# Layer 1 of a two-layer graph network: head 0's product of tile 29 through logs on ScalarE and GpSimd

## The chip, the cores and the metric

The kernel runs on one core of a Trainium2 chip. The metric is the device time of one launch in microseconds; lower is better. The engines are named as in the profile: PE (TensorE, with PEld for its weight loads), DVE (VectorE), ACT (ScalarE), POOL (GpSimd) and SP (SyncE, which here only issues transfers).

## The reference

There are 4096 nodes with 512 features, and an adjacency matrix `adj` of zeros and ones, 4096 x 4096, all in fp32. Layer 0 is a graph attention whose scores come from `h @ h.T`. Layer 1, which the change touches, has 8 heads of 64 features:

```
h = relu(layernorm(x))
data1 = (h @ W.T + b).reshape(N, 8, 64)
src = sum over d of data1 * src_proj          # one number per node and head
trg = sum over d of data1 * trg_proj
e = src[n] + trg[m]                           # per head
e = where(e >= 0, e, 0.01 * e)
e = e + adj[n, m]
scores = softmax over m of e
out[n] = sum over m of scores[n, m] * data1[m]
x = x + out
```

So a term of the softmax, before it is divided by its sum, is `exp(adj) * exp(leaky(src + trg))`.

## The kernel before

Layer 0 takes roughly the first 1.6 ms, and layer 1 the rest. In layer 1 the scores are kept transposed: neighbours `m` on the 128 partitions, nodes `n` along the free dimension, 1024 at a time (`WL`). A *group* is 1024 nodes and four of the eight heads (`HG`), so there are eight groups, 0 to 7. Inside a group the loop runs over 32 *tiles* of 128 neighbours. The order of all work is written out by hand: step `s` of the loop at the end of the kernel calls the functions in `stages`, each for a tile some steps ahead, and every engine does its instructions in the order in which they are issued.

For each tile:

- `load` (SP) fetches the 128 x 1024 block of `adj.T` into one of four buffers `e`, four steps ahead.
- `exps` (ACT, L1316) writes `exp(adj)` into `ex`, a single buffer in PSUM. It can start only when the last product of the tile before has read it.
- `last_exps` (ACT, L1326) writes `e3`, the same exponential with head 3's factor of the neighbour as bias, into SBUF.
- `weigh` (DVE) makes the products, one per head, in the order 3, 0, 1, 2 (`ORDER`). Heads 1, 2 and 3 are `max(z, g) * ex` (L1379; head 3 with `e3` in place of `ex`). Head 0 is `(rl - ngd) * ex` (L1376), where `rl` is a Relu by ACT (`relus`, L1352). Each product goes into one of two buffers of its head; head 0 has three.
- In the tiles of `BY_LOG` head 0 has no product on DVE. ACT writes the logarithm of the row factor, a Relu, into a single row buffer `lg` (`logs`, L1332); POOL adds `adj` to it in two halves of 512 columns (`add_logs`, L1341); ACT takes the Exp of that with the neighbour's factor as bias, which is head 0's product (`relus`, L1349). The first half is issued on POOL after head 3's sum two tiles earlier; the second half is issued one tile earlier and waits for head 3's product of that tile.
- The softmax's denominators: POOL adds head 3's products into `acc` (L1390). Head 0's products are added into two sums by DMAs that POOL issues (`sums`, L1360 and L1362), except in the tiles of `BY_HALF`, where POOL adds one half itself (L1396) and PE the other. Heads 1 and 2 go to PE.
- `gather` (PE) multiplies the products with the values (`pv`, L1413; first heads 3 and 0, then heads 1 and 2) and adds denominators (`dn`, L1418). At the last tile of a group it also reads the finished sums.

In groups 0 and 1 ACT also scales the values (`scale`, L1312), for the first three tiles POOL does so (L1310). In the first two thirds of a group the results of the group before are turned by PE (`pt`, L1477 and L1496), scaled by ACT and sent out.

Within a step of the loop POOL gets its work from `weigh` in this order: the DMA for the sum of the tile before, the second half of the next tile's logs, head 3's sum, the first half of the logs two tiles ahead, and the half sum of a `BY_HALF` tile. ACT gets `ex`, `e3`, then the Relu or the Exp, then the logs four tiles ahead, then the scaling.

Of the kernel before, what the change touches and what calls it, by code (L numbers as in the profile page):

```python
# [28 lines left out]
def kernel(  # L29
# [657 lines left out]
    def slot(name):  # L687
        n = taken.get(name, 0)
        taken[name] = n + 1
        return slots[name][n % len(slots[name])]  # L690
# [541 lines left out]


    PARTS = (0, 1, 2, 4, 5, 6, 8, 9, 10, 12, 13, 14, 16, 17, 18, 22)
    BY_LOG = (3, 7, 11, 15, 19, 23, 27, 31)
    BY_HALF = (4, 8, 12, 16, 20, 24, 28)
    BY_DMA = [m for m in range(NT - 1) if m not in BY_HALF]
    after = mybir.DependencyInfo(mybir.DependencyClass.Sync, mybir.DependencyReason.DATA)
# [4 lines left out]
    with tile_pool("rl") as rlp, tile_pool("zb") as zp1, tile_pool("ac") as acp, tile_pool("s1") as sp, tile_pool(  # L1243
# [85 lines left out]
        def logs(i, m, early=False):  # L1329
            if m in BY_LOG and early == (m == BY_LOG[0]):  # L1330
                r = lg_row
                nc.scalar.activation(r, us[i], AF.Relu, bias=nlg_m[:, groups[i][1], m:m + 1], scale=-(1.0 - SLOPE))  # L1332
                rl[i, m] = r

        def early_logs(i, m):
            logs(i, m, True)

        def add_logs(i, m, half, behind=None):
            if m in BY_LOG:
                cs = slice(half * BL, (half + 1) * BL)  # L1340
                add = nc.gpsimd.tensor_tensor(rl[i, m][:, cs], rl[i, m][:, cs], ra[i, m][:, cs], ALU.add)  # L1341
                if behind is not None:
                    tc.add_manual_dep(add.ins, behind.ins.name, after, reason="behind head 3's product")

        def relus(i, m):
            h = groups[i][1] * HG
            if m in BY_LOG:
                pr[i, m, 0] = slot("pr0")
# [245 lines left out]
        for s in range(len(steps)):  # L1594
            for f, ahead in stages:
                if s + ahead < len(steps):
                    f(*steps[s + ahead])
                if s == 0 and f is exps:
                    early_logs(0, BY_LOG[0])
            if s == 0:  # L1600
# [45 lines left out]
```

## Time and profile before

| | |
|---|---|
| median of 3 runs | 2763.91 us (2760.75 to 2765.06) |
| profiled execution | 2766.16 us |
| its span, first to last instruction | 2764.3 us |
| granted TensorE clock | 0.999 |
| PE busy | 2743.6 us (99%) |
| DVE busy | 2469.7 us (89%) |
| ACT busy | 1543.1 us (56%) |
| POOL busy | 1441.4 us (52%) |
| from 2025.9 to 2172.4 us (one group's length): DVE, ACT, POOL busy | 145.87, 120.74, 125.63 of 146.5 us |

Times in the profile are microseconds from the span's start. A row of the timeline gives the start, the duration, the engine, the line of the kernel, the operation, and output and inputs by the tile names in memory; several rows that follow one another are merged and counted (x2). A bracket at the end tells how long the engine was idle before it and what ended that. Many buffers of layer 1 reuse memory of layer 0, so their rows carry old names: `he_t`, `at`, `pr` and `ux` are products, Relus and adjacency blocks, `racc` the row of `src`, `rm`, `mb` and `acc_z` columns of factors. Matmuls overlap, so PE's busy time says little; the distance between their starts says more.

In the chain of waits, shares are those of the chain that ended last; "issue" is time in which an engine waited for nothing that the profile shows.

### The profile page before, as it was taken

The numbers are of one execution on the slowest core, as the hardware profiler recorded it, in microseconds if no ns is written. First come the engines' busy times: TensorE is split into PE (matmuls) and PEld (weight loads), VectorE is DVE, ScalarE is ACT, GpSimd is POOL, SyncE is SP. The second block draws the span as 40 slices with busy tenths as digits, with TensorE's granted clock in tenths as the row PEclk, the third lists the DMA queues.
The fourth block names the chain that finished last, engine by engine and source line by source line (L and its number), as shares of the span: only waits on it lengthen the run. The fifth ranks groups of instructions, "written<-read, shape, count | busy, mean of one in ns | idle before, by whom it ended". The sixth has DMA issues, their size and how long they took to land.

```text
span 2764.3 us, 49117 instructions
## 1 busy us (share of the span) xinstructions
PE 2743.6 (99%) x17903; PEld 1777.5 (64%) x17903; DVE 2469.7 (89%) x3362; ACT 1543.1 (56%) x2498; POOL 1441.4 (52%) x1236
## 2 busy tenths in 40 slices
PE   8999999999999999999999999999999999999999
PEld 5885444445888888888885433565656565655555
DVE  5767789899988888888886799999999999999998
ACT  5522233333233333433433588988888888888886
POOL 5313434444010010111108588888889897979797
PEclk9999999999999999999999999999999999999999
DMA  6627898988999999999967489999999998989897
GB/s 197 190 75 289 283 325 300 311 297 264 214 208 197 198 263 193 229 256 211 231 190 190 164 202 244 235 224 247 225 243 225 243 234 238 229 239 231 215 222 173
DMA packets 537122, 632.10 MB, mean 229 GB/s; under 512 B 292184, under 2 KB 346488, under 8 KB 536880
## 3 DMA queue, kind: packets, MB, share of 16 engines
q1 hardware_dynamic: 463600, 419.28, 50.5%
q0 software_dynamic: 71776, 206.81, 34.7%
q8 instruction: 140, 2.29, 0.3%
q10 hardware_dynamic: 1504, 2.88, 0.3%
q14 instruction: 102, 0.84, 0.1%
HBM read 406.33 MB, written 107.15 MB: 186 GB/s over the span
## 4 chain that ended last, share of the span: by engine, by line
PE 82%; DVE 7%; issue 3%; DMA 2%; POOL 2%; SPq 2%; ACT 1%; DVEq 0%; POOLq 0%; ACTq 0%
PE pv L1413 28%; PE po L841 23%; PE pe L585 12%; PE dn L1418 8%; PE bank L297 6%; DVE he_t L1379 2%; PE po L977 2%; SPq L768 2%; PE pt L1496 1%; DMA et<-er_d 1%; POOL a L989 1%; DMA a<-in_adj_t_dram 1%; PE bank L230 1%; DVE at L812 1%; PE bank L237 0%
## 5 line engine op out<-in xcount | busy, mean ns | idle before, releaser
L1413 PE MATMUL pv<-he_t,sup 128*32 128x512 f32 x6488 | 988.5, 592 | 0.9 <-DVE he_t L1379 0.9
L1413 PEld LDWEIGHTS pv<-he_t,sup 128*32 128x32 f32 x6488 | 431.8, 110 | 313.9 <-issue 111.8
L1418 PE MATMUL dn<-he_t,acc_z 128*2 128x512 f32 x1984 | 412.7, 592 | 0.0
L585 PE MATMUL pe<-he_t,he_t 128*128 128x512 f32 x896 | 386.2, 592 | 0.0
L802 ACT ACTIVATE d<-d 128x1024 f32<-128x1024 f32 x126 | 133.1, 1057 | 427.2 <-DVE d L794 226.4
L1316 ACT ACTIVATE ex<-he_t 128x1024 f32<-128x1024 f32 x255 | 262.0, 1027 | 149.3 <-DVE he_t L1379 148.2
L1390 POOL TENSOR_TENSOR acc<-acc,at 128x1024 f32<-128x1024 f32 x120 | 287.8, 2398 | 70.1 <-DVE at L1379 64.6
L1379 DVE SCALAR_TENSOR_TENSOR he_t<-z,rm,ex 128x1024 f32<-128x1024 f32 x256 | 315.2, 1271 | 0.7 <-PE dn L1418 0.2
L1379 DVE SCALAR_TENSOR_TENSOR he_t<-he_t,rm,ex 128x1024 f32<-128x1024 f32 x254 | 312.7, 1271 | 0.8 <-PE dn L1418 0.2
L585 PEld LDWEIGHTS pe<-he_t,he_t 128*128 128x128 f32 x896 | 169.3, 190 | 210.3 <-issue 194.5
L1390 POOL TENSOR_TENSOR acc<-acc,he_t 128x1024 f32<-128x1024 f32 x120 | 287.2, 2393 | 27.5 <-DVE he_t L1379 27.5
L1413 PE MATMUL pv<-at,sup 128*32 128x512 f32 x1024 | 279.9, 593 | 0.0
L841 PE MATMUL po<-sup,ux 128*128 128x256 f32 x1024 | 263.3, 379 | 0.0
L841 PE MATMUL po<-he_t,at 128*128 128x256 f32 x1024 | 263.0, 379 | 0.0
L841 PE MATMUL po<-sup,at 128*128 128x256 f32 x1024 | 242.5, 380 | 4.0 <-DVE at L812 3.8
L812 DVE TENSOR_TENSOR at<-d,a 128x1024 f32<-128x1024 f32 x126 | 154.2, 1224 | 71.4 <-PE po L841 39.7
L841 PEld LDWEIGHTS po<-sup,at 128*128 128x128 f32 x1024 | 194.0, 190 | 32.5 <-DVE at L812 6.4
L930 POOL DMA_DIRECT2D he_t<-he_t x56 | 49.4, 977 | 315.2 <-ACT he_t L844 258.9
L841 PEld LDWEIGHTS po<-he_t,at 128*128 128x128 f32 x1024 | 194.3, 190 | 27.1 <-DVE mc L591 0.3
L841 PEld LDWEIGHTS po<-sup,ux 128*128 128x128 f32 x1024 | 193.9, 190 | 26.1
L596 ACT ACTIVATE nr<-rm 128x1 f32<-128x1 f32 x144 | 29.2, 203 | 303.2 <-DVE rm L587 303.2
L590 POOL DMA_DIRECT2D er_d<-mk x136 | 75.0, 551 | 229.5 <-DVE rm L587 217.6
(348 smaller groups left out, 5481.9 us busy)
## 6 DMA issues: line engine op xcount, KB each, us to landing
he_t<-in_adj_t_dram SPq DMA_DIRECT2D x256, 512.0 KB, 6.2
acc<-he_t POOLq DMA_DIRECT2D x127, 512.0 KB, 6.8
a<-in_adj_t_dram SPq DMA_DIRECT2D x126, 512.0 KB, 5.2
acc<-pr POOLq DMA_DIRECT2D x65, 512.0 KB, 6.6
ac<-in_adj_t_dram SPq DMA_DIRECT2D x124, 256.0 KB, 5.0
ar<-in_adj_dram SPq DMA_DIRECT2D x120, 256.0 KB, 4.6
ec_d<-mc POOLq DMA_DIRECT2D x120, 256.0 KB, 4.8
er_d<-mk POOLq DMA_DIRECT2D x112, 256.0 KB, 4.6
```

What stands on the lines that cost most here:

```text
L297: nc.tensor.matmul(acc[:, j, :], w, m, start=(k == 0), stop=(k == KC // 2 - 1))
L585: nc.tensor.matmul(pe[:, :w], he_t[i][:, k, (t % TB) * P:(t % TB + 1) * P], he_t[j][:, k, BL - w:], start=(k == 0), stop=(k == KC - 1))
L590: nc.gpsimd.dma_start(er_d[rows, lo + sk:lo + w], mk[:, sk:w])
L768: nc.sync.dma_start(e[c * S:(c + 1) * S, h, 0:r * P].rearrange("p (a q) -> p a q", q=S), sq[c])
L802: nc.scalar.activation(d, d, AF.Exp)
L812: nc.vector.tensor_tensor(w, d, aj.pop((n, q)), ALU.mult)
L841: nc.tensor.matmul(acc[:, j, :], A[:, j * P:(j + 1) * P], B, start=(first_ and j == 0), stop=last, skip_group_check=True)
L1316: nc.scalar.activation(x_, ra.pop((i, m)), AF.Exp)
L1379: p_ = nc.vector.scalar_tensor_tensor(w, zs_[i, k], g_m[:, h + k, m:m + 1], e3.pop((i, m)) if k == 3 else x_, op0=ALU.max, op1=ALU.mult)
L1390: nc.gpsimd.tensor_tensor(acc[i, 3], acc[i, 3], w, ALU.add)
L1413: nc.tensor.matmul(v[c][q][col * Q:(col + 1) * Q, :], va[:, m, g * HG + k, c0:c0 + Q], pr[i, m, k][:, q * BL:(q + 1) * BL], start=(m == 0) ...
L1418: nc.tensor.matmul(dn[col * Q:col * Q + w.shape[1], :], w, src, **fl)
```

## The change

Tile 29 joins the tiles of `BY_LOG`, so that nine of the 32 tiles of each group have head 0's product made without DVE. Tile 29 follows two tiles after 27 and stands two before 31; the other tiles of the list are four apart. Tile 28 is one of `BY_HALF`.

```diff
     PARTS = (0, 1, 2, 4, 5, 6, 8, 9, 10, 12, 13, 14, 16, 17, 18, 22)
-    BY_LOG = (3, 7, 11, 15, 19, 23, 27, 31)
+    BY_LOG = (3, 7, 11, 15, 19, 23, 27, 29, 31)
     BY_HALF = (4, 8, 12, 16, 20, 24, 28)
     BY_DMA = [m for m in range(NT - 1) if m not in BY_HALF]
```

Per group, L1376 and L1352 run once less, and L1332, L1349 and L1341 (twice) run for tile 29:

```python
def add_logs(i, m, half, behind=None):
    if m in BY_LOG:
        cs = slice(half * BL, (half + 1) * BL)
        add = nc.gpsimd.tensor_tensor(rl[i, m][:, cs], rl[i, m][:, cs], ra[i, m][:, cs], ALU.add)
        if behind is not None:
            tc.add_manual_dep(add.ins, behind.ins.name, after, reason="behind head 3's product")
```

## The prediction

> **What bounds the kernel now.** I read the page's first part, then the chain of waits cut into stretches, then the groups of instructions in layer 1, and last the timeline of single engines. The profiled execution took 2766.16 us, 1.9 more than its span of 2764.3; the median of the runs shown is 2763.91. Layer 1 has eight groups (0 to 7) of 32 tiles; from tile 2 of one to tile 2 of the next, groups 2 to 7 take 146.4 to 146.7 us.
>
> Busy shares:
> ```profile
> PE 2743.6 (99%) x17903; PEld 1777.5 (64%) x17903; DVE 2469.7 (89%) x3362; ACT 1543.1 (56%) x2498; POOL 1441.4 (52%) x1236
> ```
> In layer 1 both PE and DVE look full, so shares decide nothing. The chain does, first for group 0 (1590 to 1740 us), then for 1850 to 2600 us:
> ```profile
> by line: DVE he_t L1379 38.4%; issue 17.7%; DVE he_t L1376 6.8%; DVE at L1379 6.6%; ACT at L1326 6.0%; ACT ex L1316 4.7%; ACT he_t L1326 3.6%; DVE pr L1376 3.4%; POOL lg L1341 2.6%; ACT rl L1352 2.3%; ACT ux L1352 1.5%; ACT sup L1312 1.2%;
> ```
> ```profile
> by line: PE pv L1413 75.4%; PE dn L1418 21.3%; PE pt L1496 2.9%; PE pt L1477 0.3%; issue 0.1%
> ```
> Group 0 hangs on VectorE and ScalarE; later groups are TensorE from end to end. There a tile costs PE 4.29 us (40 instructions, 0.107 us from start to start), VectorE 4.9 us with four products and 3.65 with three. VectorE runs ahead in the first half of a group and falls back in the second. In group 3 the last product of tile 30 ends at 2158.74, and the half of PE's tile that reads it starts at 2158.81: no slack is left there.
>
> **What the change removes and adds.** Per group, tile 29 loses a product (L1376) and a Relu (L1352), and gains a Relu of logs (L1332), an Exp (L1349) and two half additions (L1341):
> ```profile
> L1341 POOL TENSOR_TENSOR lg<-lg,he_t 128x512 f32<-128x512 f32 x108 | 138.6, 1283 | 21.4 <-DVE he_t L1379 21.4
> ...
> L1332 ACT ACTIVATE lg<-racc,mb 128x1024 f32<-128x1024 f32 x55 | 62.5, 1136 | 0.0
> ...
> L1352 ACT ACTIVATE rl<-z,mb,acc_z 128x1024 f32<-128x1024 f32 x45 | 55.4, 1230 | 0.0
> ...
> L1376 DVE SCALAR_TENSOR_TENSOR pr<-rl,mb,ex 128x1024 f32<-128x1024 f32 x28 | 35.6, 1270 | 1.1 <-ACT ex L1316 1.1
> ```
> VectorE: minus one product, which occupies it 1.19 us from start to start. ScalarE: plus 1.14 and 1.15, minus 1.23, so 1.06 more. GpSimd: 2 x 1.28 = 2.57 us more. TensorE and the bytes moved: unchanged. In the PE-bound groups the 1.19 us buys nothing by itself.
>
> A rule of the Trainium skill speaks against the move: GPSIMD Engine Reference, section 4.1, sends additions with two inputs to VectorE, GpSimd being about twice as slow. By these rows 2.57 against 1.19 us; if GpSimd's time were all on the path, that alone would be 8 x 1.38 = 11 us.
>
> **Where the price arises: GpSimd's additions against head 3's product.** Head 3's product reads `z` and `e3`, both in SBUF; the others read `ex`, which is in PSUM. Two places in group 1, first VectorE, then GpSimd:
> ```profile
> 1731.90 1.40 DVE L1379 SCALAR_TENSOR_TENSOR he_t<-z,rm,at 128x1024 f32<-128x1024 f32 x1
> ...
> 1736.80 2.56 DVE L1379 SCALAR_TENSOR_TENSOR at<-z,rm,he_t 128x1024 f32<-128x1024 f32 x1
> ```
> ```profile
> 1730.93 1.28 POOL L1341 TENSOR_TENSOR lg<-lg,he_t 128x512 f32<-128x512 f32 x1
> 1732.20 1.82 POOL L1310 TENSOR_SCALAR sup<-sup,acc_z 128x64 f32<-128x64 f32 x2
> ...
> 1735.86 2.40 POOL L1390 TENSOR_TENSOR acc<-acc,he_t 128x1024 f32<-128x1024 f32 x1
> ```
> (a) The product that starts at 1736.80, inside an addition that ends at 1738.26, ends at 1739.36: 1.10 after it. The one at 1731.90 ends 1.09 after the addition that runs until 1732.21. Over all 254 such products of layer 1 in the trace, "the end of the running addition plus 1.09 us, and never under 1.18 us in all" gives each duration within 0.10 us, half of them within 0.004; alone they take 1.18 to 1.28. They exclude each other. (b) The GpSimd instruction next in line lets the waiting product go first: the pair at 1732.20 takes 1.82 us, where such a one alone takes 0.44. It ends 0.1 short of its own full duration after the product.
>
> The skill's SBUF — State Buffer, section "SBUF: two separate sides", says that whoever starts first keeps the shared ports for the whole instruction. That would make the blocked product run its full 1.28 after the addition rather than 1.09; three such collisions in a group, each 0.2 us longer, would add 5 us to the sum below. The rows are used.
>
> **The chain worked through, group 3.** Before (VectorE's head 3 products of tiles 28 to 31, GpSimd, then PE at tile 30):
> ```profile
> 2144.05 1.34 DVE L1379 SCALAR_TENSOR_TENSOR he_t<-z,rm,at 128x1024 f32<-128x1024 f32 x1
> ...
> 2148.89 1.40 DVE L1379 SCALAR_TENSOR_TENSOR at<-z,rm,he_t 128x1024 f32<-128x1024 f32 x1
> ...
> 2153.78 1.38 DVE L1379 SCALAR_TENSOR_TENSOR he_t<-z,rm,at 128x1024 f32<-128x1024 f32 x1
> ...
> 2158.67 1.34 DVE L1379 SCALAR_TENSOR_TENSOR at<-z,rm,he_t 128x1024 f32<-128x1024 f32 x1
> ```
> ```profile
> 2141.90 2.40 POOL L1390 TENSOR_TENSOR acc<-acc,at 128x1024 f32<-128x1024 f32 x1 [0.45 <-DVE at L1379]
> 2144.26 0.84 POOL L1362 DMA_DIRECT2D acc<-he_t  x1
> 2145.55 2.40 POOL L1390 TENSOR_TENSOR acc<-acc,he_t 128x1024 f32<-128x1024 f32 x1 [0.44 <-DVE he_t L1379]
> 2147.92 1.28 POOL L1396 TENSOR_TENSOR acc<-acc,he_t 128x512 f32<-128x512 f32 x1
> 2150.43 2.41 POOL L1390 TENSOR_TENSOR acc<-acc,at 128x1024 f32<-128x1024 f32 x1 [1.23 <-DVE at L1379]
> ```
> ```profile
> 2157.06 3.36 PE L1413 MATMUL pv<-he_t,sup 128*32 128x512 f32 x27
> ```
> Today each addition ends just as the next head 3 product starts. Tile 27 is a short step and tile 28 has a half addition (L1396), so the new work comes where GpSimd has least room:
> 1. ScalarE's logs of 29 fit into 1.05 us of idle before tile 27's `ex`: nothing.
> 2. First half of 29 wants GpSimd at 2144.27; tile 28's head 3 has waited since 2144.05 and goes first, to 2145.39. The half ends at 2145.39 + 1.18 = 2146.57.
> 3. Queued behind it on GpSimd: tile 27's copy, 0.85 us, to 2147.37 (was 2144.26 to 2145.1); second half of 29, to 2148.61; head 3's sum (L1390) of 28, 2148.58 to 2150.98 (was 2145.55 to 2147.95).
> 4. Head 3 of 29 starts at 2148.89, now inside that sum: it ends at 2152.07, not 2150.29. ScalarE's Exp, the logs of 31 and `ex` end at 2151.75 (was 2150.03), hidden behind this. Head 1 of 29 starts at 2151.99, not 2151.40: the saved 1.19 is gone, plus 0.59.
> 5. L1396 ends at 2153.25, the sum of 29 at 2155.62; head 3 of 30, from 2154.37, ends at 2156.71 (was 2155.16).
> 6. First half of 31 goes behind it, to 2157.89; copy to 2158.7; second half to 2159.93 (was 2156.55); sum of 30, 2159.90 to 2162.30. Head 3 of 31 starts at 2160.20 inside it and ends at 2163.39 (was 2160.01).
> 7. PE, tile 30: head 0 ends at 2157.90, PE wants it at 2157.06: 0.83. Its second half, due at 2159.63, waits for head 2 until 2160.28: 0.66. Tile 31, due at 2162.90, waits for head 3 until 2163.39: 0.5. Then the sum of head 3, ready at 2165.9, wanted at 2165.6: 0.3. Together 2.3, with hand-overs 2.4 us.
>
> The next group starts with products at least 1.2 us ahead of PE and VectorE some 0.5 to 1 us later than now; where it waits for PE's buffers (tiles 11 to 19) it gets that back, and GpSimd has 3.29 + 2.57 us idle at a group's start. So the loss does not grow. In group 0 the same steps put head 3 of 31 2.85 us later, of which 2.3 to 2.4 pass to group 1 through ScalarE. Moved transfers: tile 27's, 29's and 30's copies issue 1 to 3 us later and land in 5.6 to 7.3 us, before PE reads their sums; SP's load behind the later `ex` goes 1.7 us later and has over 8. Both are costed at nothing; without that cover it would be the same microseconds.
>
> Sum: 8 x 2.4 = 19 us. On the profiled execution 2785, on the median 2783. The least known term is (b), seen only with small instructions: if the one behind loses 0.2 us less, the chain gives 13 us, with 2.5 us per sum 23.
>
> **Rivals.** *GpSimd's delay stays covered*: PE is the chain, products don't reach it late, group 0 gains 0.1: 2763.7. For it: 97% of the chain on two PE lines; against: 2.56 us at 1736.80, and GpSimd busy 15.87 of the 18.40 us from 2130.6. Chance 0.09. *VectorE is the bound*, faster: 8 x 1.19 = 9.5, 2754.4. It decides from the point where PE waits for products over 1.19 us in every group; the chain shows that in group 0 alone. Chance 0.04. *The copy of tile 26*: the Exp of 29 writes the buffer (three of them) that this copy reads. It lands 6.1 us after 2140.61, wanted at 2148.63; at the slowest landing of such copies, 10.9, the step is 2.6 us later again: 2804. Chance 0.02.
>
> **How the numbers follow.** The forecast has 0.85. Its own range is 2777 to 2787; 2771 to 2793 leaves room for half the collisions missing or one more, and leaves out the rivals. 0.2% (5.5 us) is about what a measurement of this kernel can tell from no change. Faster 0.04, same 0.09, slower 0.87.
>
> **What would show it.** Right: head 3's products of tiles 29 and 31 at about 3.2 us and of 30 at 2.3, in every group; L1341 rows of 2.3 us; groups of 148.5 to 149.2 us; PE waiting for L1379 at tiles 30 and 31. Wrong: those products still at 1.4 us (first rival if groups keep 146.4), or ScalarE waiting for a copy (the third).

## The result: 2787.3 us, 0.8% slower, and the profile after

The changed kernel takes 2787.30 us (median of 5 runs, 2784.78 to 2787.95); the kernel before, on the same chip, 2763.91. The ratio is 1.0082, 95% interval 1.0071 to 1.0093. The profiled execution took 2787.92 us with a span of 2786.1, against 2766.16 and 2764.3: 21.8 us more. The ratios here and below are formed from all runs of both kernels, and differ from the quotient of the two medians by up to 0.0006.

Busy shares of the page, and its group for the additions of the logs (count | busy us, mean ns | idle before):

```profile
PE 2759.5 (99%) x17903; PEld 1728.7 (62%) x17903; DVE 2495.1 (90%) x3354; ACT 1553.9 (56%) x2506; POOL 1478.3 (53%) x1252
...
L1341 POOL TENSOR_TENSOR lg<-lg,he_t 128x512 f32<-128x512 f32 x144 | 202.8, 1408 | 23.7 <-DVE he_t L1379 23.6
```

VectorE runs eight instructions fewer, one per group, and yet is busy 25.4 us longer. The mean of an addition of logs rose from 1286 (x128 before) to 1408 ns. Both are what two engines look like that block each other: the blocked time counts as busy.

The chain of waits in the stretch from 1850 to 2600 us, which before was PE from end to end (75.4% on L1413, 21.3% on L1418):

```profile
by line: DVE he_t L1379 24.7%; PE pv L1413 21.9%; issue 12.5%; PE dn L1418 6.4%; DVE at L1379 6.2%; DMA acc<-he_t 5.7%; DVE he_t L1376 4.5%; POOL acc L1390 3.5%; POOL lg L1341 2.9%; DVE pr L1376 2.0%; ACT at L1326 1.7%; PE pt L1496 1.2%; AC
```

PE still shows 99% busy, but the chain has left it: it now runs through VectorE's products, GpSimd's sums and the DMAs that GpSimd issues.

The place itself, in group 3. First VectorE's head 3 products of tiles 28 to 31, then GpSimd beside them (start, duration):

```profile
2150.89 1.33 DVE L1379 SCALAR_TENSOR_TENSOR he_t<-z,rm,at 128x1024 f32<-128x1024 f32 x1
...
2155.72 4.46 DVE L1379 SCALAR_TENSOR_TENSOR at<-z,rm,he_t 128x1024 f32<-128x1024 f32 x1
...
2162.49 1.30 DVE L1379 SCALAR_TENSOR_TENSOR he_t<-z,rm,at 128x1024 f32<-128x1024 f32 x1
...
2167.29 3.21 DVE L1379 SCALAR_TENSOR_TENSOR at<-z,rm,he_t 128x1024 f32<-128x1024 f32 x1
```

```profile
2148.74 2.40 POOL L1390 TENSOR_TENSOR acc<-acc,at 128x1024 f32<-128x1024 f32 x1 [0.43 <-DVE at L1379]
2151.11 2.27 POOL L1341 TENSOR_TENSOR lg<-lg,he_t 128x512 f32<-128x512 f32 x1
2153.32 0.85 POOL L1362 DMA_DIRECT2D acc<-he_t  x1
2153.93 1.56 POOL L1341 TENSOR_TENSOR lg<-lg,he_t 128x512 f32<-128x512 f32 x1
2155.20 2.65 POOL L1390 TENSOR_TENSOR acc<-acc,he_t 128x1024 f32<-128x1024 f32 x1
2157.56 1.53 POOL L1396 TENSOR_TENSOR acc<-acc,he_t 128x512 f32<-128x512 f32 x1
2160.32 2.39 POOL L1390 TENSOR_TENSOR acc<-acc,at 128x1024 f32<-128x1024 f32 x1 [1.24 <-DVE at L1379]
```

At 2151.11 the first half of the new addition starts while the product of 2150.89 waits; the product goes first and the half takes 2.27 us instead of 1.28. That is the handover that the prediction used. At 2155.72 tile 29's product meets the sum of tile 28, which ends at 2155.20 + 2.65 = 2157.85. But here the half sum L1396 follows without letting the product in, until 2157.56 + 1.53 = 2159.09, and the product ends at 2155.72 + 4.46 = 2160.18, 1.09 after that. In groups 2 to 7 this product takes 4.44 to 4.47 us, in each. Groups 0 and 1 differ: there tile 29's product takes 1.31 us, and the collisions lie at tile 28 (2.13 and 2.15), tile 30 (1.84 and 1.83) and tile 31 (3.18 and 3.20).

What PE waits for at tile 31 of the same group (its weight loads; idle time before them in brackets):

```profile
2170.55 0.11 PEld L1413 LDWEIGHTS pv<-at,sup 128*32 128x32 f32 x2 [0.41 <-DVE at L1379]
...
2173.09 0.15 PEld L1418 LDWEIGHTS dn<-acc,mb 128*2 128x2 f32 x6 [0.71 <-POOL acc L1390]
```

and in the table of waits for 1850 to 2600 us (us in total, times, longest):

```profile
PEld dn L1418 <- POOL acc L1390: 3.8, 5, 1.0
...
PEld dn L1418 <- DMA acc<-he_t: 2.0, 2, 1.0
...
PEld dn L1418 <- DMA acc<-pr: 1.0, 1, 1.0
```

So the group's end waits in turn for head 3's product, for its sum on GpSimd and, in three of the five groups of this stretch, for the DMA that adds tile 30's head 0. From tile 2 of one group to tile 2 of the next, by the starts of VectorE's head 3 products, it is 148.7 us for group 0 and 149.4 to 150.0 for the others, without a trend; before it was 146.4 for group 0, 147.5 for group 1, and 146.3 to 146.7 for the others.

### The profile page after: what moved, and what is told of

Its sections match the earlier page's. It is cut to its first block, busy times and chain, and to the rows that moved or that the text cites. A ratio compares the mean times of both kernels' runs of the same rounds, so it can differ in the third digit from the quotient of the medians.

```text
span 2786.1 us, 49107 instructions
## 1 busy us (share of the span) xinstructions
PE 2759.5 (99%) x17903; PEld 1728.7 (62%) x17903; DVE 2495.1 (90%) x3354; ACT 1553.9 (56%) x2506; POOL 1478.3 (53%) x1252
## 4 chain that ended last, share of the span: by engine, by line
PE 52%; DVE 21%; issue 8%; POOL 7%; ACT 6%; DMA 5%; SPq 2%; DVEq 0%; POOLq 0%; ACTq 0%
PE po L841 23%; PE pe L585 12%; DVE he_t L1379 11%; PE pv L1413 6%; PE bank L297 5%; DVE at L1379 2%; PE po L977 2%; POOL lg L1341 2%; DVE he_t L1376 2%; PE dn L1418 2%; DMA acc<-he_t 2%; POOL acc L1390 2%; SPq L768 1%; ACT at L1326 1%; DMA a<-in_adj_t_dram 1%
## 5 line engine op out<-in xcount | busy, mean ns | idle before, releaser
L1413 PE MATMUL pv<-he_t,sup 128*32 128x512 f32 x6488 | 984.8, 593 | 6.3 <-DVE he_t L1379 5.6
L1413 PEld LDWEIGHTS pv<-he_t,sup 128*32 128x32 f32 x6488 | 404.2, 110 | 346.1 <-issue 153.7
L1418 PE MATMUL dn<-he_t,acc_z 128*2 128x512 f32 x1984 | 405.2, 592 | 0.0
L1413 PE MATMUL pv<-at,sup 128*32 128x512 f32 x1024 | 275.3, 593 | 0.0
L1341 POOL TENSOR_TENSOR lg<-lg,he_t 128x512 f32<-128x512 f32 x144 | 202.8, 1408 | 23.7 <-DVE he_t L1379 23.6
```

Source lines behind the costliest of these rows:

```text
L1413: nc.tensor.matmul(v[c][q][col * Q:(col + 1) * Q, :], va[:, m, g * HG + k, c0:c0 + Q], pr[i, m, k][:, q * BL:(q + 1) * BL], start=(m == 0) ...
L1418: nc.tensor.matmul(dn[col * Q:col * Q + w.shape[1], :], w, src, **fl)
```

## The experiments

The theory, P: GpSimd's additions and head 3's product exclude each other, and VectorE's delay reaches PE. The rivals differ by run. Every time is a median, set against the kernel before on the same chip (2765.77 us for the first four runs, 2766.80 for the next four, 2763.89 for the last two).

**The move without the additions.** Tile 29's head 0 still goes through logs and Exp, but nothing is added on GpSimd for it.

```diff
-            if m in BY_LOG:
+            if m in BY_LOG and m != 29:
                 cs = slice(half * BL, (half + 1) * BL)
```

> The changed kernel without GpSimd's two half additions for tile 29; this leaves adj out of head 0's product of that tile. ScalarE's two new instructions and VectorE's saved product stay. Theory P (GpSimd's additions hold up head 3's products at the shared SBUF ports): head 3's products of tiles 29 and 31 fall from 4.46 and 3.21 us to 1.3 to 1.4, groups return to 146.4 us, time 2763 (2759 to 2767). Rival S (ScalarE, with 1.06 us more per tile and one long queue, brings ex late): stays near 2787, since ScalarE's work is unchanged; at least above 2775.

Measured: 2769.56 us, ratio 1.0009 (1.0001 to 1.0018). Tile 29's head 3 takes 1.42 us and tile 30's 1.34, but tile 31's still collides:

```profile
2155.92 3.23 DVE L1379 SCALAR_TENSOR_TENSOR at<-z,rm,he_t 128x1024 f32<-128x1024 f32 x1
```

VectorE, 1.2 us earlier for the product it no longer makes, now reaches tile 31 inside the sum of tile 30 (2155.38 to 2158.06). By the starts of its tiles, PE loses 0.4 to 0.7 us at tile 31 in groups 2 to 5, 1.65 in group 1 and nothing in groups 0 and 6; its largest waits there are for the DMAs of head 0 (5.4 us from 1850 to 2600 us), not for the product (1.5). The time lies 2.6 us above what P expected. So the product that VectorE is spared buys nothing, and moving one engine earlier makes a collision by itself.

**The additions without the move.** The kernel before, with two half additions at the same places that write where nobody reads.

```diff
-            if m in BY_LOG:
+            if m in BY_LOG or m == 29:
                 cs = slice(half * BL, (half + 1) * BL)
-                add = nc.gpsimd.tensor_tensor(rl[i, m][:, cs], rl[i, m][:, cs], ra[i, m][:, cs], ALU.add)
+                row = ra[i, m][:, cs]
+                to, by = (rl[i, m][:, cs],) * 2 if m in BY_LOG else (slots["o"][0], row)
+                add = nc.gpsimd.tensor_tensor(to, by, row, ALU.add)
```

> The kernel before, with two half additions of 512 columns on GpSimd at the places where tile 29's stand, into a buffer that nobody waits for; tile 29's product stays on VectorE. Theory P: slower although nothing depends on the result, with head 3's products of tiles 28 to 31 lengthened as in the changed kernel and VectorE keeping its 1.19 us: 2790 (2780 to 2800). Rival S: nobody on ScalarE waits for these, so 2764 (2760 to 2768).

Measured: 2784.84 us, ratio 1.0067 (1.0055 to 1.0080). Nothing reads what these additions write, so the 19.1 us can only be what they take from others. Tile 29's head 3, in group 3:

```profile
2154.01 3.93 DVE L1381 SCALAR_TENSOR_TENSOR at<-z,rm,he_t 128x1024 f32<-128x1024 f32 x1
```

This is the one collision here: it takes 3.93 to 3.96 us in every group, while tiles 28, 30 and 31 stay at 1.3 (once 1.63), against the expectation. The two halves of the change give 3.8 and 19.1 us, together 22.9; the change itself 23.4. Their collisions are not those of the change, so the agreement of the sum proves little.

**Head 3's product with one SBUF input.** The changed kernel, with `e3` of tiles 28 to 31 replaced by a PSUM buffer that ScalarE fills at tile 26 (`from_psum` gives it out for all of them). GpSimd's work stays.

```diff
+                    if k == 3 and m == 26:
+                        ps_[i] = p_t.tile([P, BL], FP, name="pt"); nc.scalar.copy(ps_[i], x_[:, 0:BL])
                     p_ = nc.vector.scalar_tensor_tensor(w, zs_[i, k], g_m[:, h + k, m:m + 1],
-                                                        e3.pop((i, m)) if k == 3 else x_,
+                                                        from_psum(i, m) if k == 3 and m > 27 else e3.pop((i, m)) if k == 3 else x_,
```

> The changed kernel, but head 3's products of tiles 28 to 31 take their second input from a PSUM buffer that ScalarE fills once per group at tile 26 (0.58 us), so those products use a stale exponential; sizes and all of GpSimd's work are the same. Theory P: products of 1.27 us whatever GpSimd does, no loss: 2764 (2760 to 2769). Rival Q (GpSimd's queue being late is enough: head 3's sum and the copies reach PE late at the group's end): the queue's own work is unchanged, so most of the loss stays, 2778 to 2787. Rival S: 2785 or more.

Measured: 2777.22 us, ratio 1.0040 (1.0028 to 1.0053). Tile 29's product now runs through the whole meeting with GpSimd's sum at full speed (VectorE, then GpSimd):

```profile
2152.21 1.27 DVE L1386 SCALAR_TENSOR_TENSOR at<-z,rm,pt 128x1024 f32<-128x1024 f32 x1
```

```profile
2150.75 2.66 POOL L1397 TENSOR_TENSOR acc<-acc,he_t 128x1024 f32<-128x1024 f32 x1
2153.11 1.53 POOL L1403 TENSOR_TENSOR acc<-acc,he_t 128x512 f32<-128x512 f32 x1
```

All products of tiles 28 to 31 take 1.27 to 1.28 us. The Trainium skill's SBUF — State Buffer, section "Who interferes with whom", says that a VectorE instruction with two SBUF inputs contends with a GpSimd instruction that reads SBUF, and one with at most one SBUF input, outside the 2-port performance modes, does not; 4.46 against 1.27 us agrees. But 11.5 us of loss remain, where P expected none, and at the group's end PE waits far longer for DMAs than in the changed kernel, where it was 3.0 us in all (1850 to 2600 us):

```profile
PEld dn L1425 <- DMA acc<-he_t: 7.4, 4, 2.7
...
PE dn L1425 <- DMA acc<-he_t: 4.3, 3, 1.8
PEld dn L1425 <- DMA acc<-pr: 3.8, 3, 3.1
```

**The same, with short DMAs.** In addition, the DMAs that add tiles 29 and 30 carry 64 of 1024 columns.

```diff
-                nc.gpsimd.dma_start(acc[i, 0, (len(BY_DMA) + BY_DMA.index(m)) % 2], pr[i, m, 0], accum_op=ALU.add)
+                cs = slice(0, 64 if m > 28 else WL)
+                nc.gpsimd.dma_start(acc[i, 0, (len(BY_DMA) + BY_DMA.index(m)) % 2][:, cs], pr[i, m, 0][:, cs], accum_op=ALU.add)
```

> The kernel in which head 3's products of tiles 28 to 31 read PSUM (2777 us), with the short copies of tiles 29 and 30 as well. There the products are 1.27 us long and PE waits at tile 31 alone, 0.9 to 3.0 us per group, while copies land 8 to 11 us after their issue. If the copies are what is left: 2766 (2763 to 2769). Rival S (ScalarE's ex of tile 29 comes 0.9 us late and VectorE waits for it): stays at 2775 to 2778.

Measured: 2766.50 us, ratio 1.0002 (0.9993 to 1.0011), the time of before. The chain from 1850 to 2600 us is PE's again:

```profile
by line: PE pv L1421 75.0%; PE dn L1426 21.1%; PE pt L1504 2.9%; PE pt L1485 0.2%; issue 0.2%; DVE he_t L1387 0.2%; ACT at L1326 0.1%; ACT ex L1316 0.1%; ACT he_t L1349 0.1%; DVE rd L1490 0.0%; DVEq L1387 0.0%; DVEq L1382 0.0%
```

With ports and DMAs both out of the way, the added work on ScalarE and GpSimd costs nothing. The two causes together are the whole loss.

**Short DMAs alone**, in the changed kernel (the same edit).

> The changed kernel, but the copies of tiles 29 and 30 into head 0's sums carry 64 of 1024 columns (the rest of these two tiles is left out of the denominators). GpSimd still issues both; they land sooner. In the changed kernel PE also waits at the group's end for the copy of tile 30 (landing 7.1 to 8.5 us after its issue). Theory P with the copies as a second, smaller term: head 3's products stay at 4.46 and 3.21 us, PE's wait at tile 31 shrinks by 0.5 to 1 us per group: 2781 (2777 to 2786). Rival Q (late copies carry most of the loss): 2770 or less. If copies are hidden: 2786 to 2788.

Measured: 2789.86 us, ratio 1.0080 (1.0067 to 1.0094): no gain, a miss. PE no longer waits for a DMA at the group's end, but for head 3's sum as before, and then for the last group's results at the start of the next:

```profile
PEld pt L1497 <- DVE rd L1483: 6.4, 5, 1.7
PEld pv L1414 <- ACT os L1467: 6.2, 10, 0.9
...
PEld dn L1419 <- POOL acc L1391: 3.8, 5, 1.0
```

The first two rows were 3.5 and 2.5 us in the changed kernel. By the starts of PE's tiles, the loss at tile 31 falls from 1.40 to 1.25 us (mean of groups 2 to 6), and tiles 0 to 2 of the groups that follow lose 0.11 us more. The DMA is only the last of several late things; without the collision's delay PE waits for it still, as the run with PSUM shows.

**No half sum behind tile 28.** The changed kernel with 28 out of `BY_HALF`: L1396 goes, and tile 28 gets a DMA.

```diff
-    BY_HALF = (4, 8, 12, 16, 20, 24, 28)
+    BY_HALF = (4, 8, 12, 16, 20, 24)
```

> The changed kernel with tile 28 out of BY_HALF, so that its part of the sum goes by a DMA as for other tiles: 1.28 us less of additions and 0.85 us of DMA issue on GpSimd, and one matmul less on PE. Theory P: tile 29's head 3 product is held by one addition instead of two, 3.2 us instead of 4.46; the time falls by about 1 us per group to 2779 (2773 to 2784). Rival S: no change beyond the matmul, 2785 to 2788.

Measured: 2789.03 us, ratio 1.0081 (1.0068 to 1.0095). Tile 29's head 3 fell to 3.22 us as expected; the time did not fall, a miss. The Exp of tile 31 writes the buffer that tile 28's new DMA reads, and waits for it:

```profile
ACT he_t L1349 <- DMA acc<-he_t: 8.7, 3, 3.2
ACT pr L1349 <- DMA acc<-pr: 5.7, 2, 2.9
```

PE also waits for products at tiles 24 to 27 already, where the changed kernel lost nothing (0.7 to 1.3 us in groups 3 to 6); why is not shown. Other waits took the place of the one removed, so the run does not tell what the longer collision costs. The run below that moves the half sum does.

**29 in place of 27.** The kernel before with eight tiles by logs, as before, and no more work on any engine.

```diff
-    BY_LOG = (3, 7, 11, 15, 19, 23, 27, 31)
+    BY_LOG = (3, 7, 11, 15, 19, 23, 29, 31)
```

> The kernel before with tile 29 in place of tile 27 in the list: eight tiles through logs per group, as before, so the same work on every engine. Theory P, worked through by the same steps: tile 28's half sum still stands before tile 29's head 3, and 29 and 31 crowd the additions, so head 3's products of tiles 29 to 31 collide: groups of 148.4 to 148.9 us, 2780 (2772 to 2786). Rival N (the ninth tile's extra work is what costs, not its place): 2764 (2760 to 2768).

Measured: 2780.84 us, ratio 1.0056 (1.0043 to 1.0069); groups of 148.3 to 148.6 us, but for 149.6 in group 1. The collisions are at tiles 30 and 31; tile 29, where one was expected too, stays at 1.3. In group 3:

```profile
2157.74 2.27 DVE L1379 SCALAR_TENSOR_TENSOR he_t<-z,rm,at 128x1024 f32<-128x1024 f32 x1
...
2163.51 3.19 DVE L1379 SCALAR_TENSOR_TENSOR at<-z,rm,he_t 128x1024 f32<-128x1024 f32 x1
```

With no ninth tile, the place alone makes 14.0 us.

**A DMA in place of the two additions.** In the changed kernel, tile 29's logs get `adj` by one DMA with addition, issued at tile 27.

```diff
+            if m == 27:
+                nc.gpsimd.dma_start(rl[i, 29], ra[i, 29], accum_op=ALU.add)
```

> The changed kernel with tile 29's two half additions on GpSimd replaced by one accumulating DMA of the same 512 KB, issued by GpSimd (0.85 us) at tile 27. It uses no port of an engine. Theory P: head 3's product of tile 29 at 1.4 us, tile 31's perhaps 3.2 us, as in the run without additions (2764.0 us span): 2768 (2764 to 2774), the Exp perhaps waiting 0 to 1 us for the landing of 6 to 7 us. Rival S or Q (any later hand-over of the row costs as much): 2780 or more.

Measured: 2794.24 us, ratio 1.0102 (1.0088 to 1.0115): a miss, the slowest of all. The collisions are nearly gone (in group 3 1.81 us for tile 28, 1.39 for tile 29), but the Exp waits for the DMA:

```profile
2160.28 1.15 ACT L1349 ACTIVATE pr<-lg,t_m 128x1024 f32<-128x1024 f32 x1 [5.18 <-DMA lg<-he_t]
```

It was issued at 2150.03, so it took 10.2 us until the Exp could start. `ex` of the next tile is queued behind that Exp on ScalarE, and VectorE stood still 3.96 us for it.

**The half sum moved behind tile 29's product.** No work is taken out; L1396 of tile 28 is issued one step later on GpSimd, so that nothing is queued between the sum of 28 and the product.

```diff
                         add_logs(i, m + 1, 1, p_)
+                        if m == 29:
+                            late = nc.gpsimd.tensor_tensor(acc[i, 0, 2], acc[i, 0, 2], pr[i, 28, 0][:, BL:], ALU.add)
+                            tc.add_manual_dep(late.ins, p_.ins.name, after, reason="behind head 3's product")
...
-            elif m in BY_HALF:
+            elif m in BY_HALF and m != 28:
```

> The changed kernel, with one GpSimd instruction moved: the half sum of tile 28 (L1396) is issued behind head 3's product of tile 29 instead of right behind the sum of tile 28, so that no second addition is queued when that product waits. All work stays. Theory P, with the handover as the timeline shows it: head 3's product of tile 29 falls from 4.46 to 3.2 us, that of tile 30 is hit in its place (2.2 to 2.3 us instead of 1.30), that of tile 31 stays at 3.2; groups of 148.8 to 149.1 us instead of 149.7; 2783 us (2779 to 2786), some 5 us under the changed kernel. Rival K: what is taken from one collision comes back in the next, and the amount of GpSimd work at the end of the group sets the price: three collisions of other sizes, but groups of 149.5 and 2787 us as the changed kernel.

Measured: 2785.22 us, ratio 1.0071 (1.0057 to 1.0085). Head 3 of tiles 29 to 31:

```profile
2155.45 3.21 DVE L1379 SCALAR_TENSOR_TENSOR at<-z,rm,he_t 128x1024 f32<-128x1024 f32 x1
2160.96 2.48 DVE L1379 SCALAR_TENSOR_TENSOR he_t<-z,rm,at 128x1024 f32<-128x1024 f32 x1
2166.94 3.18 DVE L1379 SCALAR_TENSOR_TENSOR at<-z,rm,he_t 128x1024 f32<-128x1024 f32 x1
```

These are close to the prediction's own 3.2, 2.3 and 3.2. The groups take 149.2 to 149.9 us from group 1 on, nearer to rival K's 149.5 than to P's 148.8 to 149.1, and the time is 21.3 us over before against the change's 23.4; the intervals overlap. So most of what one collision loses the next one gains, as K had it: the three products take 8.87 us here and 8.97 in the changed kernel. The size of the single collision was wrong in the prediction, their sum was nearly right.

**Tile 13 as the ninth**, in the middle of the group.

```diff
-    BY_LOG = (3, 7, 11, 15, 19, 23, 27, 29, 31)
+    BY_LOG = (3, 7, 11, 13, 15, 19, 23, 27, 31)
```

> The ninth tile is 13 instead of 29, in the middle of the group, between 11 and 15; all else as in the changed kernel, and tile 12 also has a half sum on GpSimd. Theory P: the same collisions come about at tiles 13 to 15, head 3's product 3 us and more there, and VectorE, which lies behind from there on, meets GpSimd's later additions too: groups of 148.5 to 150.5 us, 2784 to 2795 us. Rival E: VectorE has more slack in the middle of a group than at its end, and makes up for the collisions before PE needs the products: groups of 146.5 to 147 us, 2764 to 2768 us.

Measured: 2787.96 us, ratio 1.0082 (1.0069 to 1.0094), groups of 149.3 to 150.6 us from group 1 on. There is no room in the middle either; tile 14's head 3 in group 3 (4.13 to 4.74 us in groups 1 to 7):

```profile
2089.85 4.17 DVE L1379 SCALAR_TENSOR_TENSOR he_t<-z,rm,at 128x1024 f32<-128x1024 f32 x1
```

After it the collisions stop (in groups 1 to 7 tiles 15 to 31 are at 1.3 to 1.4 us again, once at 1.64), but VectorE does not make up its delay: by the starts of its tiles PE loses 0.4 to 0.75 us at tiles 13 to 15 of groups 1 to 7, and 2.1 to 2.7 us more from tile 22 to tile 30.

## Why the prediction was right, and which terms were not

- **The mechanism held**, with a second cause that the prediction had put at nothing, the late DMAs. Take the additions away: 1.0009. Add them alone: 1.0067. Take away the second SBUF input and the late DMAs: 1.0002. The first rival (the delay stays covered) and the second (VectorE the bound) are out; of the third, a wait for tile 26's DMA, the trace of after shows none.
- **The sum.** 19 us were predicted, 21.8 in the profiled executions and 23.4 in the medians; 2787.3 is inside the stated 2771 to 2793 and just above the narrower 2777 to 2787. Groups 0 and 1 lost 2.2 us each, near the 2.3 to 2.4 that the prediction had for group 0, though with the collisions at other tiles than it wrote; groups 2 to 6 lost 3.2 on average instead of 2.4. There is no growth from group to group, as predicted.
- **Steps 1 to 3** came out as written in group 3: the first half let the product go first and took 2.27 us (2144.27 to 2146.57 in the prediction), then the 0.85 us issue, the second half and the sum of 28. L1341's rows of 2.3 us are there.
- **Step 4 failed, and with it step 5.** Term (b), that the next instruction on GpSimd lets the waiting product in, was named the least known. It failed for L1396: tile 29's product took 4.46 us, not 3.2. For the same reason tile 30 did not collide, 1.30 and not 2.3. Tile 31's 3.2 was right (3.21). The groups, 149.4 to 150.0 us, lie above the 148.5 to 149.2 that it gave as a sign. The two errors nearly cancel: from tile 28 to the start of tile 31 PE loses 1.5 to 1.8 us in groups 2 to 6 (by the starts of its tiles), against 1.5 predicted, and 1.5 to 1.8 with L1396 out of the way. That the sum came out near is thus in part luck.
- **Step 7's last terms were too small**; this is most of the miss. At tile 31 the prediction had 0.5 us for head 3's product and 0.3 for its sum, 0.8 together. Measured are 0.41 and 0.71 in the rows above, and 1.2 to 1.6 us for the tile as a whole, the wait for the DMA included.
- **"Moved transfers at nothing" was wrong for one of them.** The DMA that adds tile 30 lands 7.1 to 8.5 us after its issue, before 6.0 to 7.3 (the last group's 4.8 and 4.9 left out), and PE waits for it up to 1.0 us in three of the five groups of the stretch. The prediction's 5.6 to 7.3 us for the three copies was a misreading too: in the trace of before tile 27's takes 7.9 in group 3, and 7.0 to 8.7 over all groups. The prediction did give the price of a missing cover, "the same microseconds"; that cover was gone. Its share in the changed kernel alone is small, since shortening it and tile 29's gained nothing there; with the collisions removed the two are worth 11.8 us (from 11.5 over before to 0.3 under it).
- **"The 1.19 us buys nothing"** held: the move alone is not faster.

What stays open: why the DMA of tile 30 takes longer to land than before.

## What to carry to other kernels

Where an engine is full to the microsecond, price a new instruction on its neighbour by what it shuts out, not by what it waits for: two additions whose result nobody read cost 19 us, of the 23 of the whole change. Lay the two engines' timelines side by side at the step itself and look for instructions with two SBUF inputs that will meet; shares of busy time (GpSimd 52%) say nothing of that. And where the late piece is one of several that end at nearly the same time, taking away one of them may show nothing: here short DMAs alone gave nothing back and the PSUM input alone about half; ports and DMAs had to go together before all the time came back.

## What the runs showed of the hardware

Who gets the ports next, when a product of VectorE and a further addition of GpSimd both wait, went by how early the further addition starts. Take, over all twelve traces, the head 3 products with both inputs in SBUF that start during one addition of GpSimd while a second addition follows it at once. The second addition starts 0.03 to 0.06 us before the end of the first in 97 such meetings, and the product went first in all of them; it starts 0.28 to 0.50 us before that end in 27, and the additions went first in all of those. All 27, and none of the 97, stand in an unbroken run of GpSimd instructions behind the issue of a DMA: the rows of 1.56, 2.65 and 1.53 us above follow the 0.85 us of L1362 and each overlap the one before by 0.24 to 0.29 us (2153.93 against 2153.32 + 0.85; 2157.56 against 2155.20 + 2.65). L1396 itself shows both cases: behind tile 28 in the changed kernel it kept the product out, and behind tile 12 in the run with tile 13 (group 3, 2085.88 us), with no early start, it gave way and took 2.27 us. Why the early starts come behind a DMA's issue isn't shown here, nor whether the early start is the cause or goes along with it.
